# Layer 1's attention weights: six of eight blocks transposed in 32x32 squares on VectorE and moved by ScalarE and SyncE

## The chip, the cores and the metric

The kernel runs on one core of a Trainium2 chip. The core has five engines that work side by side, each through its own instructions in order: TensorE (PE, with its weight loads PEld), VectorE (DVE), ScalarE (ACT), GpSimd (POOL) and SyncE (SP), which here only issues transfers and relays signals. Sixteen DMA engines carry out the transfers that SP, ACT and POOL issue. The metric is the device time of one execution in microseconds (us), lower is better. Before the change it is 2416.36 us, the median of three runs (2415.96 to 2419.54).

## What is computed

The input is eight images of 256 channels and 1024 positions, all in float32. Layer 0 is eight-head attention with an output projection. Layer 1 works on the tokens t (1024 x 256 per image): first attention with one head and a residual, then a mixture of eight experts with two per token. The change is in layer 1's attention:

```python
t = t + _L1_attn_ref(_ln_t(t), L1_attn_W)

def _L1_attn_ref(x, W):
    xa = jnp.einsum('bnd,ed->bne', x, W)
    scores = jnp.einsum('bne,bme->bnm', xa, x)
    attn = jax.nn.softmax(scores, axis=-1)
    y = jnp.einsum('bnm,bmd->bnd', attn, x)
    return y
```

The softmax is over m, and the last product sums over m too. TensorE sums over the partitions, so a block of exponentials that was computed with n on the partitions must be turned, to have m there, before it can enter the last product.

## The kernel before, in words

The main loop takes the images one after the other. For each, `layer0` does the eight-head attention, `attend` does layer 1's attention, and `normed` with `dispatch` normalises, routes the tokens to experts and scatters them to DRAM. For the eighth image (b = 7) there is a difference: ahead of its `attend` the experts' products of the first seven images are computed, and during its `attend` and its own experts (`dense`) the results of the other seven are gathered from DRAM by POOL, added by DVE, turned by DVE and stored by SP (class `Results`, its places in `PLACES`).

`attend` normalises t to n1 (L645), turns it to nT (L648) and multiplies by W to xa (L655). Then it goes over eight blocks i of 128 tokens:

- `scores(i)`: four matmuls of 128x512 write the scores ps of block i to a PSUM tile (L670); DVE takes the negated row maximum nmax (L678); ACT writes the exponentials ex and their row sums to SBUF (L681). The ex tiles come from the pool `expp`, six buffers that share the tag "exps" with layer 0's exponentials.
- `mix(i)`: eight transposes of 128x128 on TensorE write the turned block pa to PSUM (L689); DVE copies it to SBUF as aT (L691); eight matmuls of 128x256 give py (L695); DVE scales by the reciprocal of the row sums and adds the residual (L699, L701).

The blocks are pipelined by one: `scores(i + 1)` is written ahead of `mix(i)`. The PSUM tiles ps and pa come from one pool of three (`ps_big`). Two calls of `fill` in the last block put pieces of the next image's projections (pv, pqk; L387, L328) into the stream, so that TensorE has work in the last waits; for b = 7 they are places of `Results`.

A scheduler places the instructions of each engine by its own estimates and adds the semaphores; it splits and interleaves groups. So before the change TensorE's stream in a middle block is: two matmuls of ps, eight of pa, two of the next ps, eight of py. What stands on SP's queue around `attend` is the load of later images (xT, L93; xs, L427) and the store of t (L1327).

Of the kernel before, what the change touches and what calls it, by code (L numbers as in the profile page):

```python
# [10 lines left out]
F32 = mybir.dt.float32  # L11
# [8 lines left out]
def kernel(  # L20
# [23 lines left out]
    nc = tc.nc  # L44
    P = 128
    B, C, S = x.shape
    E, D, FF = w1.shape
# [4 lines left out]
    NT = S // P  # L52
# [15 lines left out]
    expp = ctx.enter_context(tc.tile_pool(name="expp", bufs=6))  # L68
# [6 lines left out]
    def big(name):  # L75

        return ps_big.tile([P, 1024], F32, tag="big", name=name)

    def acc(name):

        return ps_acc.tile([P, 512], F32, tag="acc", name=name)
# [54 lines left out]
    for e in range(E):  # L136
# [30 lines left out]
        fill=0.0,  # L167
# [42 lines left out]
    SQ = 32  # L210
    NQ = P // SQ
# [40 lines left out]
    def layer_norm(t, dst, eps, name):  # L252
        return Norm(t, dst, eps, name).blocks(0, NT)

    def to_channels(t, dst, name):

        for cc in range(NCC):
            pt = big(f"pt_{name}_{cc}")
            for i in range(NT):
                nc.tensor.transpose(pt[:, ts(i, P)], t[:, i, ts(cc, P)], ident)  # L260
            copied = nc.vector.tensor_copy(dst[:, cc, :], pt)
        return copied
# [380 lines left out]
    def attend(b, t1, fill, tick=nothing):  # L643
        n1 = one.tile([P, NT, D], F32, tag="n", name=f"n1_{b}")
        layer_norm(t1, n1, 1e-5, f"a{b}")  # L645
        fill("norm 1")
        nT = one.tile([P, NCC, S], F32, tag="nT", name=f"nT_{b}")
        to_channels(n1, nT, f"n1_{b}")  # L648
        fill("normed 1")
        xa = one.tile([P, NCC, S], F32, tag="xa", name=f"xa_{b}")  # L650
        for ec in range(NCC):
            px = big(f"px_{b}_{ec}")
            for dc in range(NCC):
                for n in range(NH2):
                    nc.tensor.matmul(  # L655
                        px[:, ts(n, 512)],
                        WT[:, dc, ts(ec, P)],
                        nT[:, dc, ts(n, 512)],
                        start=(dc == 0),
                        stop=(dc == NCC - 1),  # L660
                    )
            tick(("xa", ec), nc.vector.tensor_copy(xa[:, ec, :], px))

        t2 = t1

        def scores(i):
            psc = big(f"ps1_{b}_{i}")
            for ec in range(NCC):
                for n in range(NH2):
                    nc.tensor.matmul(  # L670
                        psc[:, ts(n, 512)],
                        xa[:, ec, ts(i, P)],
                        nT[:, ec, ts(n, 512)],
                        start=(ec == 0),
                        stop=(ec == NCC - 1),
                    )
            nmax = small.tile([P, 1], F32, tag="nmax", name=f"nmax_{b}_{i}")
            tick(("max", i), nc.vector.tensor_reduce(nmax, psc, AX.X, ALU.max, negate=True))  # L678
            ex = expp.tile([P, 1024], F32, tag="exps", name=f"ex1_{b}_{i}")
            ssum = small.tile([P, 1], F32, tag="ssum", name=f"ssum_{b}_{i}")  # L680
            nc.scalar.activation(ex, psc, AF.Exp, bias=nmax, scale=1.0, accum_out=ssum)  # L681
            return ex, ssum

        def mix(i, ex, ssum):
            if i == NT - 1:
                fill("last weights")
            pt = big(f"pa_{b}_{i}")
            for m in range(NT):
                nc.tensor.transpose(pt[:, ts(m, P)], ex[:, ts(m, P)], ident)  # L689
            aT = two.tile([P, S], F32, tag="tr", name=f"aT_{b}_{i}")  # L690
            nc.vector.tensor_copy(aT, pt)  # L691
            ahead = fill("last products") if i == NT - 1 else None
            py = acc(f"py_{b}_{i}")
            for m in range(NT):
                nc.tensor.matmul(  # L695
                    py[:, :D], aT[:, ts(m, P)], n1[:, m, :], start=(m == 0), stop=(m == NT - 1)
                )
            rs = small.tile([P, 1], F32, tag="rs1", name=f"rs1_{b}_{i}")
            nc.vector.reciprocal(rs, ssum)  # L699
            with tc.issue_after(ahead.ins) if ahead else nullcontext():  # L700
                mixed = nc.vector.scalar_tensor_tensor(  # L701
                    t2[:, i, :], py[:, :D], rs, t1[:, i, :], ALU.mult, ALU.add
                )
            tick(("mixed", i), mixed)

        pending = None
        for i in range(NT):
            now = (i, *scores(i))
            if pending is not None:
                mix(*pending)  # L710
            pending = now
        mix(*pending)
        return t2


# [87 lines left out]
    def normed(b, t2, fill, tick=nothing, norm=None):  # L803

        if norm is None:
            n2 = one.tile([P, NT, D], F32, tag="n", name=f"n2_{b}")
            tick("normed", layer_norm(t2, n2, 1e-5, f"f{b}"))
        else:
            n2 = norm.dst
            tick("normed", norm.blocks(NT - 1, NT))  # L810
        fill("norm 2")
        nT = one.tile([P, NCC, S], F32, tag="nT", name=f"n2T_{b}")
        tick("turned", to_channels(n2, nT, f"n2_{b}"))

        nc.gpsimd.tensor_add(t2, t2, n2)  # L815
        fill("normed 2")
        l = logits(b, nT)
        return n2, nT, l
# [260 lines left out]
    class Results:  # L1079
# [94 lines left out]
        def tick(self, place, behind=None):  # L1174
            added, sent, stored = self.PLACES.get(place, (0, 0, 0))
            if added:
                with tc.issue_after(behind.ins):
                    for _ in range(added):
                        self.add()
            for _ in range(sent):  # L1180
                self.gather(behind)
            for _ in range(stored):
                if self.whole:
                    b, total, n = self.whole.pop(0)
                    store(b, total, n)
# [130 lines left out]
    for b in range(B):  # L1316
        xT = next_x
        if b + 1 < B:
            next_x = load_x(b + 1)
        if b > 0:  # L1320
            xs = load_squares(b)
        t1 = layer0(b, xT, begun, routing, xs)
        if b + 1 < B:
            begun = Begin(b + 1, next_x)
            t2 = attend(b, t1, begun.at)
            n2, _, l = normed(b, t2, begun.at)
            nc.sync.dma_start(groups[0].sums[b], t2)  # L1327
            routing = dispatch(b, n2, l, groups[0])
            continue
        experts(groups[0])  # L1330
        others = Results(groups[0])
        others.begin()
        norm = None

        def fill(place):

            nonlocal norm
            others.tick(place)
            if place == "last products":
                norm = Norm(t1, one.tile([P, NT, D], F32, tag="xa", name=f"n2_{b}"), 1e-5, f"f{b}")  # L1340
                return norm.blocks(0, NT - 1)

        t2 = attend(b, t1, fill, others.tick)
        dense(b, t2, norm, others.tick)
        assert others.added == len(others.units) and not others.whole
# [42 lines left out]
```

## Time and profile before

| What | Value |
|---|---|
| time, median of 3 | 2416.36 us |
| the profiled execution's own time | 2397.03 us |
| its span, first to last instruction | 2395.3 us |
| TensorE busy | 2353.9 us (98%) |
| VectorE, ScalarE, GpSimd busy | 64%, 39%, 18% |
| mean granted TensorE clock | 0.996 |
| DMA packets, data | 114778, 196.59 MB |

The profile shows one execution. Rows name the line, the engine, the operation and the tiles (out<-in), the shapes and the count, then the busy time and the mean of one, then the idle time ahead of them and what ended most of it. Float32 matmuls of this kernel appear as two MATMUL records each, the transposes as one. Records of matmuls overlap, so the pace of a group is read from the starts of its neighbours, not from the mean of one. The chain of waits is the work that ended last, followed back step by step. The profiled execution is 19 us shorter than the median of the timed runs; sums from the profile are differences and are put onto the median.

### The profile page before, as it was taken

To read this page: it belongs to the slowest core of one execution; us is meant where nothing else is said; L and a number is where in the kernel's file an instruction comes from. 1 tells how busy PE (TensorE), PEld (TensorE's weight loads), DVE (VectorE), ACT (ScalarE), POOL (GpSimd) and SP (SyncE) were. 2 spreads that over 40 slices of the span, in tenths; PEclk is the share of its full clock that TensorE was granted. 3 is DMA by queue.
4 is the path that set the end of the run, shared out by engine and by line. 5 is a ranking of instruction groups with operands and counts; after the bars stand their busy time and mean duration, and the time that the engine had idled before them with its cause. 6 is when DMAs were issued, how large, how long until landed. Compare 5 with 4: busy or idle time off the path is not lost.

```text
span 2395.3 us, 36813 instructions
## 1 busy us (share of the span) xinstructions
PE 2353.9 (98%) x13759; PEld 1313.9 (55%) x13759; DVE 1541.2 (64%) x3660; ACT 938.0 (39%) x1570; POOL 420.4 (18%) x391
## 2 busy tenths in 40 slices
PE   9999999999999999999999999999999999999898
PEld 3356534654466336633664356435653388887565
DVE  5775587457845785578647864787468763334776
ACT  3651266126611662156315641465136612221111
POOL 0000012000200020003000200020002234444663
PEclk9999999999999999999999999999999999999999
DMA  8993201010101010001000100100010256664454
GB/s 294 386 386 106 53 19 36 1 36 12 43 1 36 8 47 1 18 18 54 1 18 18 47 8 3 34 25 12 1 36 19 76 176 220 219 215 162 148 172 119
DMA packets 114778, 196.59 MB, mean 82 GB/s; under 512 B 15752, under 2 KB 58408, under 8 KB 112808
## 3 DMA queue, kind: packets, MB, share of 16 engines
q1 hardware_dynamic: 88504, 126.52, 16.0%
q0 software_dynamic: 25008, 67.20, 9.1%
q8 instruction: 109, 1.79, 0.3%
q10 hardware_dynamic: 1088, 0.52, 0.1%
q14 instruction: 69, 0.57, 0.1%
HBM read 108.88 MB, written 110.90 MB: 92 GB/s over the span
## 4 chain that ended last, share of the span: by engine, by line
PE 90%; DVE 5%; DMA 2%; ACT 1%; issue 1%; POOL 0%; SPq 0%; DVEq 0%; ACTq 0%; POOLq 0%
PE po L545 19%; PE psc L468 18%; PE py L695 8%; PE ps L670 7%; PE pqk L350 7%; PE pr L636 5%; PE pv L387 4%; PE ph L1025 4%; PE pe L1050 4%; PE pdh L1254 2%; PE px L655 2%; PE pdy L1278 2%; PE pa L689 2%; PE pqk L328 2%; PE px L1015 1%
## 5 line engine op out<-in xcount | busy, mean ns | idle before, releaser
L509 ACT ACTIVATE ex<-psc,nmax 128x1024 f32<-128x1024 f32 x512 | 570.5, 1115 | 304.1 <-DVE scrap L492 220.4
L468 PE MATMUL psc<-qk,qk 64*64 64x512 f32 x4096 | 577.4, 593 | 10.3 <-ACT ex L509 10.3
L545 PE MATMUL po<-ex,vs 64*64 64x512 f32 x4096 | 573.2, 592 | 1.3 <-DVE vs L525 0.3
L492 DVE TENSOR_SCALAR_CACHE_REDUCE scrap<-psc,nmax 128x512 f32<-128x512 f32 x512 | 384.5, 751 | 149.0 <-PE psc L468 121.8
L483 DVE TENSOR_REDUCE nmax<-psc 128x1 f32<-128x512 f32 x512 | 350.7, 685 | 9.3 <-PE psc L468 9.3
L468 PEld LDWEIGHTS psc<-qk,qk 64*64 64x64 f32 x4096 | 180.7, 132 | 285.9 <-ACT ex L509 138.3
L545 PEld LDWEIGHTS po<-ex,vs 64*64 64x64 f32 x4096 | 177.6, 132 | 273.0 <-issue 81.2
L695 PE MATMUL py<-n,aT 128*128 128x256 f32 x1024 | 236.3, 384 | 2.9 <-DVE aT L691 2.9
L670 PE MATMUL ps<-nT,xa 128*128 128x512 f32 x512 | 236.0, 592 | 0.0
L695 PEld LDWEIGHTS py<-n,aT 128*128 128x128 f32 x1024 | 190.5, 190 | 66.1 <-DVE aT L691 41.8
L888 POOL DMA_INDIRECT rows<-n,d_at x112 | 108.8, 972 | 654.4 <-DVE nmax L483 654.1
L681 ACT ACTIVATE ex<-ps,nmax 128x1024 f32<-128x1024 f32 x64 | 71.3, 1115 | 348.0 <-DVE nmax L678 333.5
L815 POOL TENSOR_TENSOR t<-t,n 128x2048 f32<-128x2048 f32 x8 | 36.3, 4532 | 924.0 <-DVE n L242 924.0
L350 PE MATMUL pqk<-xT,wqkv 128*128 128x512 f32 x384 | 171.2, 599 | 0.0
L701 DVE SCALAR_TENSOR_TENSOR t<-py,rs,t 128x256 f32<-128x256 f32 x64 | 30.9, 483 | 192.7 <-PE py L695 192.7
L670 PEld LDWEIGHTS ps<-nT,xa 128*128 128x128 f32 x512 | 93.5, 190 | 81.2 <-issue 75.1
L350 PEld LDWEIGHTS pqk<-xT,wqkv 128*128 128x128 f32 x384 | 71.0, 190 | 99.9 <-issue 77.8
L1134 POOL DMA_INDIRECT yk<-y,yat x112 | 111.0, 991 | 70.1 <-issue 27.1
L636 PEld LDWEIGHTS pr<-wo,res 128*128 128x128 f32 x512 | 120.7, 331 | 3.7 <-ACT res L563 3.7
L636 PE MATMUL pr<-wo,res 128*128 128x256 f32 x512 | 121.6, 398 | 0.3 <-ACT res L563 0.3
L387 PE MATMUL pv<-wqkv,xT 128*128 128x512 f32 x256 | 120.3, 599 | 1.2 <-DVE v L395 1.0
L315 ACT ACTIVATE qk<-pqk,b_qks 128x512 f32<-128x512 f32 x124 | 85.6, 691 | 88.9 <-PE pqk L350 79.8
(189 smaller groups left out, 2477.8 us busy)
## 6 DMA issues: line engine op xcount, KB each, us to landing
rows<-wb SPq DMA_DIRECT2D x7, 8192.0 KB, 51.7
y<-yb SPq DMA_DIRECT2D x63, 256.0 KB, 2.3
xs<-in_x_dram SPq DMA_DIRECT2D x64, 128.0 KB, 4.0
out_dram<-oT SPq DMA_DIRECT2D x60, 128.0 KB, 2.9
xT<-in_x_dram SPq DMA_DIRECT2D x7, 1024.0 KB, 4.8
sums<-t SPq DMA_DIRECT2D x7, 1024.0 KB, 3.9
o<-sums SPq DMA_DIRECT2D x7, 1024.0 KB
wpack<-in_L_ffn_w_dram SPq DMA_DIRECT2D x4, 1024.0 KB
```

What stands on the lines that cost most here:

```text
L350: mm = nc.tensor.matmul(pq[:, ts(n, 512)], wqkv[:, cc, t, ts(g, P)], xT[:, cc, ts(n, 512)], start=(cc == 0), stop=(cc == NCC - 1),)
L387: nc.tensor.matmul(pv, self.xT[:, cc, ts(i, P)], wqkv[:, cc, 2, :], start=(cc == 0), stop=(cc == NCC - 1),)
L468: mm = nc.tensor.matmul(pss[at, h][ts(c, DK), ts(n, 512)], k[r, j * P + c * DK : j * P + (c + 1) * DK], q[r, ts(n, 512)], start=True, stop ...
L483: firsts[at, h] = nc.vector.tensor_reduce(nmax, pss[at, h][:, ts(0, 512)], AX.X, ALU.max, negate=True)
L492: seconds[h] = nc.vector.tensor_scalar(scrap, pss[at, h][:, ts(1, 512)], -1.0, nmaxes[at, h], ALU.mult, ALU.min, accum_out=nmax,)
L509: nc.scalar.activation(ex, pss.pop((at, h)), AF.Exp, bias=nmaxes.pop((at, h)), scale=1.0, accum_out=sums[at][:, h : h + 1],)
L545: mm = nc.tensor.matmul(po[n][ts(h, DK), :], vss[at][keys, h, :], exps[at, h][keys, ts(n, 512)], start=(j == 0 and turn == 0), stop=(j == ...
L636: nc.tensor.matmul(pr[:, :C], own(res[:, g, :], i), wo[:, g, :], start=(g == 0), stop=(g == NPAIR - 1))
L670: nc.tensor.matmul(psc[:, ts(n, 512)], xa[:, ec, ts(i, P)], nT[:, ec, ts(n, 512)], start=(ec == 0), stop=(ec == NCC - 1),)
L695: nc.tensor.matmul(py[:, :D], aT[:, ts(m, P)], n1[:, m, :], start=(m == 0), stop=(m == NT - 1))
L888: scatter = nc.gpsimd.indirect_dma_start(out=view[:, :], out_offset=bass.IndirectOffsetOnAxis(ap=ats[k][:, i : i + 1], axis=0), in_=n2[:, ...
L1134: ins = nc.gpsimd.indirect_dma_start(out=self.slot(at)[:, k, :], out_offset=None, in_=self.group.y[:, :], in_offset=bass.IndirectOffsetOnAxis(
```

## The change

For the blocks 1 to 6, `turn` takes the place of TensorE's transposes. VectorE turns each 32x32 square of the 128x1024 block in place among the squares (`nc.vector.transpose`, into sq). That leaves each square turned inside, but in the wrong group of 32 partitions. Sixteen moves per block then bring the squares to their places in aT, each from 32 partitions to 32 partitions, 8 runs of 32 floats (128 B) per partition: eight are copies on ACT, eight are transfers issued by SP. sq and aT are two more tiles of the pool `expp`. Blocks 0 and 7 keep the old way (`turn_now`). The order of writing changes too: the product of block i is written two blocks behind its scores instead of one, block 0's after the scores of block 2, and the last three products (5, 6, 7) stand after the scores of block 7, with `fill("last weights")` after product 5 and block 7's transposes ahead of product 6.

```diff
-        def mix(i, ex, ssum):
-            if i == NT - 1:
-                fill("last weights")
+        def turn(i, ex):
+            sq = expp.tile([P, S], F32, tag="exps", name=f"sq_{b}_{i}")
+            nc.vector.transpose(sq, ex)
+            aT = expp.tile([P, S], F32, tag="exps", name=f"aT_{b}_{i}")
+            to = aT.rearrange("p (m a q) -> p a m q", a=NQ, q=SQ)
+            since = sq.rearrange("p (m k q) -> p k m q", k=NQ, q=SQ)
+            for a in range(NQ):
+                for k in range(NQ):
+                    move = nc.sync.dma_start if (a + k) % 2 else nc.scalar.copy
+                    move(to[ts(k, SQ), a], since[ts(a, SQ), k])
+            return [aT[:, ts(m, P)] for m in range(NT)]
+
+        def turn_now(i, ex):
             pt = big(f"pa_{b}_{i}")
             for m in range(NT):
                 nc.tensor.transpose(pt[:, ts(m, P)], ex[:, ts(m, P)], ident)
             aT = two.tile([P, S], F32, tag="tr", name=f"aT_{b}_{i}")
             nc.vector.tensor_copy(aT, pt)
+            return [aT[:, ts(m, P)] for m in range(NT)]
+
+        def mix(i, aT, ssum):
             ahead = fill("last products") if i == NT - 1 else None
             py = acc(f"py_{b}_{i}")
             for m in range(NT):
                 nc.tensor.matmul(
-                    py[:, :D], aT[:, ts(m, P)], n1[:, m, :], start=(m == 0), stop=(m == NT - 1)
+                    py[:, :D], aT[m], n1[:, m, :], start=(m == 0), stop=(m == NT - 1)
                 )
...
-        pending = None
+        pending = []
         for i in range(NT):
-            now = (i, *scores(i))
-            if pending is not None:
-                mix(*pending)
-            pending = now
-        mix(*pending)
+            ex, ssum = scores(i)
+            if 0 < i < NT - 1:
+                ex = turn(i, ex)
+            pending.append((i, ex, ssum))
+            if i == 2:
+                first, ex, ssum = pending.pop(0)
+                mix(first, turn_now(first, ex), ssum)
+            elif i > 2:
+                mix(*pending.pop(0))
+        fill("last weights")
+        (last, ex, ssum) = pending.pop()
+        ex = turn_now(last, ex)
+        mix(*pending.pop())
+        mix(last, ex, ssum)
```

NQ is 4 and SQ is 32. In the changed kernel L688 is the square transpose, L695 the moves, L702 and L704 the old transposes and their copy, L711 the products.

## The prediction

> **What bounds the kernel now.** I read the chain of waits of the whole page first. TensorE carries 90% of it, and the transposes that the change takes out (pa, L689) are 2%.
>
> ```profile
> PE 90%; DVE 5%; DMA 2%; ACT 1%; issue 1%; POOL 0%; SPq 0%; DVEq 0%; ACTq 0%; POOLq 0%
> ```
>
> Then the chain inside one `attend` (second image; start, duration in us, engine, tile, line, count):
>
> ```profile
> 448.23 3.45 PE ps L670 x8
> 451.70 1.24 DVE nmax L678
> 453.00 1.28 ACT L681
> 454.30 1.21 ACT ex L681 x2
> 455.56 1.09 PE pa L689 x8
> 456.65 1.72 PE ps L670 x4
> 458.37 3.45 PE py L695 x16
> 461.82 1.72 PE ps L670 x4
> 463.54 0.87 PE pa L689 x8
> 464.41 1.72 PE ps L670 x4
> 466.13 3.58 PE py L695 x16
> ```
>
> From the second block on only TensorE is in it. A block takes 7.89 us (pa at 463.54, 471.42 and 479.31): 0.87 pa, 3.44 ps, 3.58 py. The stretch from the first ps (448.23) to the end of the last py (515.18) is 66.95 us. So TensorE time removed here is time of the end, if nothing later takes its place.
>
> Third, the groups that serve as prices:
>
> ```profile
> L434 DVE STREAM_TRANSPOSE t<-xs 128x1024 f32<-128x1024 f32 x16 | 32.0, 2060 | 0.0
> L681 ACT ACTIVATE ex<-ps,nmax 128x1024 f32<-128x1024 f32 x64 | 71.3, 1115 | 348.0 <-DVE nmax L678 333.5
> ```
>
> A square transpose of a whole block costs 2.06 us; ScalarE idles 348 us ahead of its 64 exponentials, so it has room. Fourth, the transfers. The eight xs loads at 503 us have the shape of one block's transfers (8 transfers, 256 packets each), but 512 B packets from HBM; the second line is the half microsecond from 10.0 us, which holds only packets of 256 B or less (mostly b_v):
>
> ```profile
> q1 hardware_dynamic: 2176, 1.05, 57.3%
> q1 hardware_dynamic: 396, 0.10, 88.1%
> 502.99 3.76 SPq L427 DMA_DIRECT2D xs<-in_x_dram  x8
> ```
>
> A packet's engine time: 0.573 x 10 us x 16 engines / 2176 = 42 ns at 512 B; 0.881 x 0.5 x 16 / 396 = 17.8 ns at 256 B. Issuing: 3.76 / 8 = 0.47 us each.
>
> **What the Trainium skill says.** "VectorE: DVE Perf Modes", The three transpose paths: VectorE turns only 32x32 blocks, so the squares must still be moved; the kernel's own L434 and L1190 agree, since they store by quadrant. "ScalarE: Activation LUTs", Table sets: copies are in every set, so the copies cost no table load; the trace agrees (res copies stand among exponentials without one). "DMA: Bandwidth & Descriptors", Specifications: below 512 B a transfer does read-modify-write; the same page, Why small descriptors are slow (HBM only), says SBUF to SBUF does not suffer. The 17.8 ns speak against a penalty on reading small packets, but no transfer from SBUF to SBUF is in this trace: this is the largest unknown.
>
> **The change part by part.** I place the changed program's TensorE order for the second to seventh image on a clock (ps 3.45 us, py 3.45, pa 0.87, a pv of two matmuls 1.72): ps0, ps1, ps2, pa0, 3/4 ps3, py0, 1/4 ps3, 1/4 ps4, py1, 3/4 ps4, py2, ps5, py3, ps6, py4, ps7, py5, pv2, pa7, py6, pv3, py7.
>
> *Removed from TensorE*: six pa, 6 x 0.87 = 5.2 us; the start bubble (from 451.70 to 455.56 are 3.86 us, of which ps1 hides 3.45), 0.4 us; and 0.13 us that a py takes longer behind its copy, seven times, 0.9. Check: 8 x 3.45 + 8 x 3.45 + 2 x 0.87 + 2 x 1.72 = 60.4 against 66.95, 6.5 us less.
>
> *Added waits on TensorE*: py of a turned block now waits for eight transfers, mostly landed. For the price of landed waits: VectorE's first n of an image waits for eight landed scatters and starts 0.20 us after the reciprocal ends (435.85 to 436.05), without them 0.03 (266.76 to 266.79). 0.17 x 6 = 1.0 us, behind which the rest of py and the next ps queue. I charge it all; it is nothing if TensorE's queue runs ahead.
>
> *VectorE*: the copy of pa (1.22) goes, a transpose (2.06; 1.1 if the contiguous form ran at the copy's pace per element) comes. Per block: 1.22 nmax + 2.06 + 0.16 + 0.48 + 0.43 + 0.18 = 4.5 us, hidden under TensorE's 6.9.
>
> *ScalarE*: eight copies of 32 x 256. lT's copy of 256 elements took 0.373 us; two res copies in a row 1.06 against 0.59 for one, so in a row one costs 0.12 less. 0.37 + 7 x 0.26 = 2.2 to 8 x 0.40 = 3.2 us (0.40: the SBUF-to-SBUF wqkv copy of 512 elements, 0.614, less 256 x 0.83 ns, the rate of the "ScalarE: Activation LUTs" page); I take 2.5. The exponentials of the next block queue behind these copies, which wait for sq, which waits for this block's exponentials: a loop of 1.30 + 2.06 + 2.5 + 0.15 = 6.0 us (6.7 at the upper end), under TensorE's 6.9. Cover gone, every us above 6.9 is paid in five blocks.
>
> *Transfers*: 8 issues of 0.47 = 3.8 us per block on an otherwise waiting SP queue; the xs loads behind them need ps7 anyway. Engines: 2176 packets / 16 = 136 each, 2.4 us at 17.8 ns, 5.7 at 42. I take 30 ns, 4.1 us, hidden. Landing: 2.3 us (the median of y's stores, 256 KB) to 4.7 (xs); with seven issues ahead the last lands 5.6 us after sq.
>
> *Latency of a block*, from the end of ps: 0.2 + 1.23 nmax, 1.3 ex, 2.06 sq, 5.6, hand-overs 0.15: 10.5 us. On the clock ps3 ends at 18.1 and py3 starts at 31.9: 13.8 us. 3.3 to spare, of which VectorE's order (nmax behind the previous sq, a scaling and a statistic) and ScalarE's (ex behind copies) eat about 2. For a few first blocks the margin is 1 us; I charge 0.6 us per image.
>
> *Buffers*: ex, sq and aT rotate through the six of `expp`; some copies of ScalarE wait for the transfers that read sq two blocks earlier, landed by then. PSUM gets freer.
>
> So per image 6.5 - 1.0 - 0.6 = 4.9, six images: 29.4 us. *First image*: here VectorE's fourth transpose stands behind the scaling of py1, after ps6, and SP is held until 211.4 us by the packing of weights (sq of block 1 is ready at about 209.5); I take 2 of the 4.9 (0 to 5). *Last image*: POOL's gathers and SP's stores already use 53% of the DMA engines from 2185 to 2262 us, and VectorE is busy 57.4 of 77 us; six transposes instead of copies add 5. At 30 ns the transfers would need 4.1 / 0.47 = 8.7 us per block against 7.9: a loss of some 5, less its saving of 4.9. I take +1 (-5 to +25). Sum: -29.4 - 2 + 1 = -30.4. The profiled execution would span 2365 us; on the median, 2386.
>
> **The rivals.**
> *Transfers by rate, slower.* If a 128 B packet costs more, the transfers set the pace. sq1 is ready at 11.8 us on the clock; 48 transfers of 17 packets per engine, then 1.2 landing, py6, pv3, py7: the image ends at 21.6 + 816p us. It exceeds 66.95 from p = 56 ns. For: the skill's read-modify-write. Against: 17.8 and 42 ns. At 74 ns (twice the 37 ns of the final 512 B stores: 0.211 x 12 x 16 / 1088) it ends at 82.0, +15 per image, +120: 2536. Place: TensorE before py1 to py6.
> *Transfers by latency, nothing left.* ps of block k to py of block k spans two blocks. If the last lands 3 us later than I take it, the loop is 10.5 + 2 + 3.3 = 15.8, 7.9 us per block, as before: 2416. For: xs landed up to 8.3 us after issue. Against: those read HBM, in a queue.
> *ScalarE as the bound, half the gain.* At 0.50 us per copy the loop is 1.30 + 2.06 + 4.0 + 0.15 = 7.5, 0.6 above 6.9 in five blocks: 3.0 of the 4.9 are lost. 30.4 - 18 = 12.4: 2404. Against: every copy row in the trace.
> That the transposes are not gone is excluded: the changed program's TensorE list has two pa per image.
>
> **How the numbers follow.** Likeliest case 0.58 (2370 to 2400), ScalarE 0.12 (2400 to 2411), latency 0.08 (2412 to 2421), rate 0.14 (2425 to 2600), transfers late enough in latency or in the last image to lose 5 to 40 us 0.08. A difference under 0.2%, 4.8 us, can't be told from none in this kernel. Faster 0.58 + 0.12 = 0.70, same 0.08, slower 0.22. The range goes from 2369 (upper bounds: every image 6.5 us, 0.04 below) to 2450, which takes in the late cases and the first part of the rate case and leaves some 0.14 above; the likeliest case alone is 2370 to 2400.
>
> **What would show it.** Right: `attend` of the middle images about 62 us from first ps to last py; TensorE idle before L711 under 1 us per block; ScalarE moves at 0.3 to 0.4 us; some 104,000 more packets (48 x 2176) at 20 to 42 ns. Wrong: idle of TensorE before L711 ended by transfers (rate if the DMA row reads 9 in `attend`, latency if it reads 5 or less), or idle before ps ended by ex (ScalarE's loop). A last image over 10 us longer would be the collision with gathers.

## The result and the profile after

The changed kernel takes 2383.74 us (median of 4 runs, 2381.21 to 2386.16), the kernel before 2416.16 us (2415.91 to 2419.54): ratio 0.986, 95% interval 0.985 to 0.988, 32 us less. The forecast was 2386. The time agrees; below, several of its terms don't.

The chain of waits of the whole page, kernel after. TensorE still carries 90%. A share that was not there before is put down to another core or an unknown queue, although the program runs on one core; the experiments come back to it:

```profile
PE 90%; DVE 5%; DMA 1%; issue 1%; ACT 1%; another core or an unknown queue 1%; SPq 0%; DVEq 0%; ACTq 0%; POOLq 0%
```

The chain inside one `attend`, second image, kernel after (start, duration in us, engine, tile, line, count):

```profile
447.28 10.30 PE ps L670 x24
457.58 0.87 PE pa L702 x8
458.46 2.58 PE ps L670 x6
461.03 3.45 PE py L711 x16
...
475.69 3.43 PE ps L670 x8
479.12 3.45 PE py L711 x16
482.57 3.43 PE ps L670 x8
486.00 3.45 PE py L711 x16
```

From the first ps on, TensorE alone is in it. A block is 3.43 + 3.45 = 6.88 us instead of 7.89, with nothing between the two. Measured on TensorE's timeline from the first ps to the end of the last py, the stretch is 60.44 us in each of the six middle images, against 67.12 before.

The groups that replace the prices of the forecast: first the new ScalarE copies (busy us, mean ns, idle before them), then the instructions that write sq (ns min/median/max), then those that write aT by transfer (time to issue one, same columns).

```profile
L695 ACT COPY aT<-sq 32x256 f32<-32x256 f32 x384 | 154.4, 402 | 77.3 <-DVE sq L688 47.4
```

```profile
L688 DVE STREAM_TRANSPOSE sq<-ex x48: 1210/1245/1334, 207.2 to 2208.9; 128x1024 f32<-128x1024 f32 x48
```

```profile
L695 SPq DMA_DIRECT2D aT<-sq x384: 4/609/1707, 212.7 to 2214.7; - x192
```

The contiguous transpose costs 1.245 us, not the 2.06 us of the rows that store by quadrant; a copy 0.402 us, with 3.30 us for eight in a row, so they do not overlap; an issue 0.61 us in the median, with 0.65 us from one to the next. And the DMA row of the same image from 458 to 494 us (busy tenths of the 16 engines, then packets, MB and share):

```profile
DMA  0224324032422223324302242240031423401224
...
q1 hardware_dynamic: 12238, 1.48, 27.0%
```

0.270 x 36 us x 16 engines / 12,238 packets = 12.7 ns per packet of 128 B, under the lower end (17.8) of the forecast. No slice of the row reads above 4: the engines are far from full.

### The profile page after: what moved, and what is told of

It reads as the page before. It is cut to its first block, busy times and chain, and to the rows that moved or that the text cites. A ratio compares the mean times of both kernels' runs of the same rounds, so it can differ in the third digit from the quotient of the medians.

```text
span 2382.3 us, 37255 instructions
## 1 busy us (share of the span) xinstructions
PE 2316.6 (97%) x13375; PEld 1280.4 (54%) x13375; DVE 1537.0 (65%) x3660; ACT 1091.7 (46%) x1954; POOL 421.7 (18%) x391
## 4 chain that ended last, share of the span: by engine, by line
PE 90%; DVE 5%; DMA 1%; issue 1%; ACT 1%; another core or an unknown queue 1%; SPq 0%; DVEq 0%; ACTq 0%; POOLq 0%
PE po L545 19%; PE psc L468 19%; PE py L711 9%; PE ps L670 9%; PE pqk L350 7%; PE pr L636 5%; PE pv L387 4%; PE ph L1052 4%; PE pe L1077 4%; PE pdy L1305 2%; PE px L655 2%; PE pdh L1281 2%; PE pqk L328 2%; PE px L1042 1%
## 5 line engine op out<-in xcount | busy, mean ns | idle before, releaser
L509 ACT ACTIVATE ex<-psc,nmax 128x1024 f32<-128x1024 f32 x512 | 570.0, 1114 | 306.8 <-DVE scrap L492 220.3
L711 PE MATMUL py<-n,aT 128*128 128x256 f32 x1024 | 234.2, 382 | 5.5 <-DVE aT L704 4.6
L670 PE MATMUL ps<-nT,xa 128*128 128x512 f32 x512 | 228.8, 592 | 0.2
L711 PEld LDWEIGHTS py<-n,aT 128*128 128x128 f32 x1024 | 195.9, 192 | 56.6 <-issue 24.0
L695 ACT COPY aT<-sq 32x256 f32<-32x256 f32 x384 | 154.4, 402 | 77.3 <-DVE sq L688 47.4
L678 DVE TENSOR_REDUCE nmax<-ps 128x1 f32<-128x1024 f32 x64 | 78.0, 1219 | 84.9 <-PE ps L670 80.4
```

The lines of the kernel that those rows point to most:

```text
L509: nc.scalar.activation(ex, pss.pop((at, h)), AF.Exp, bias=nmaxes.pop((at, h)), scale=1.0, accum_out=sums[at][:, h : h + 1],)
L670: nc.tensor.matmul(psc[:, ts(n, 512)], xa[:, ec, ts(i, P)], nT[:, ec, ts(n, 512)], start=(ec == 0), stop=(ec == NCC - 1),)
L695: move(to[ts(k, SQ), a], since[ts(a, SQ), k])
L711: nc.tensor.matmul(py[:, :D], aT[m], n1[:, m, :], start=(m == 0), stop=(m == NT - 1))
```

## The experiments

Each kernel left a trace, and the differences between images are finer there than in the total. The table cuts each profiled execution at the first ps of an image (us): the first image, the mean of the second to sixth (to the next image's first ps), the seventh (up to the last image's first ps), and from there to the end.

| kernel | first | 2nd to 6th | seventh | last to end | median of runs | ratio to before, 95% |
|---|---|---|---|---|---|---|
| before (the execution that the forecast read) | 250.3 | 248.1 | 503.0 | 203.8 | 2416.2 | |
| before_again | 250.3 | 248.1 | 504.9 | 216.9 | 2412.1 | 1.000 (0.9995 to 1.0012) |
| after_again | 250.7 | 241.4 | 496.8 | 227.5 | 2380.1 | 0.986 (0.984 to 0.987) |
| order_only | 249.6 | 247.3 | 505.6 | 219.8 | 2409.1 | 0.997 (0.996 to 0.998) |
| half | 245.9 | 244.7 | 500.6 | 219.0 | 2389.6 | 0.990 (0.988 to 0.992) |
| last_old | 249.5 | 241.4 | 495.9 | 218.4 | 2372.0 | 0.983 (0.981 to 0.985) |
| last_old2 | 249.5 | 241.4 | 496.6 | 219.1 | 2371.6 | 0.983 (0.982 to 0.984) |
| last_dve | 249.5 | 241.4 | 497.8 | 221.1 | 2374.0 | 0.984 (0.983 to 0.985) |
| last_sp | 249.3 | 241.4 | 498.3 | 227.3 | 2379.4 | 0.986 (0.985 to 0.988) |
| last_actq | 249.5 | 241.4 | 497.2 | 220.3 | 2374.8 | 0.984 (0.983 to 0.985) |
| act12 | 247.2 | 246.3 | 504.0 | 225.9 | 2405.1 | 0.996 (0.994 to 0.997) |
| sp12 | 254.2 | 249.2 | 506.8 | 230.3 | 2435.5 | 1.008 (1.007 to 1.010) |
| deep3_7 | 257.8 | 247.5 | 503.5 | 222.2 | 2416.8 | 1.001 (1.000 to 1.002) |

### Order or transposes: order_only and half

order_only writes the products two blocks behind the scores, with every block transposed by TensorE; half moves blocks 1, 3 and 5 in squares in that order. The added lines of the loop (the removed ones and its end left out):

```diff
+            if waiting is not None:
+                j, jex, jsum = waiting
+                pending.append((j, turn_now(j, jex), jsum))
+                waiting = None
+            if i in ():            # half: (1, 3, 5)
+                pending.append((i, turn(i, ex), ssum))
+            else:
+                waiting = (i, ex, ssum)
+            if i >= 2:
+                mix(*pending.pop(0))
...
```

> All eight blocks transposed by TensorE, as before the change, but written in the changed order: the transposes one block behind the scores, the products two blocks behind. Theory (the gain is the TensorE time of the transposes): only the start bubble and the 0.13 us per product go, 1.3 us per image, 8 images: 9 to 11 us faster than before, 2406. Rival (the gain is the deeper order, which hides the chain of maximum, exponential and copy): more than half of the 32 us, 2400 or less.

> Blocks 1, 3 and 5 moved in squares, blocks 0, 2, 4, 6 and 7 by TensorE, in the order of order_only. Theory: three of six transposes of 0.87 us are gone, so the time lies midway between order_only and the changed kernel: about 2395. Rival (order): the same as order_only and as the changed kernel within 5 us. If the moves themselves cost TensorE something that grows with their density, it lies nearer to the changed kernel than midway, 2388 or less.

order_only is 2409.1 us, 7 less than before on that chip (2415.9), not the 9 to 11 expected: the deeper order is a small part. The stretch of a middle image goes 67.12 (before), 66.38 (order_only), 63.75 (half), 60.44 (after): 0.74 for the order, then 2.63 for the first three transposes, 0.88 each, which is the 0.87 us of the pa row. The last three give 3.31: 2.6 for themselves, and 0.65 at the first pa. In order_only and half it stands behind the scores of block 1, idles 0.43 us for its exponential and takes 1.09 us; in the changed kernel it stands behind the scores of block 2, without a wait, and takes 0.87. So the saving in the middle images is mainly TensorE time of transposes, and it adds up block by block. In total time half did not lie midway (2395) but at 2389.6. The table says where: in the six middle images it saves less than after_again, in the first and in the last more. Something at both ends charges for the squares.

### The same kernels once more: after_again and before_again

Both kernels as they are.

> The changed kernel once more, nothing edited. It asks whether VectorE's idle times in the last image (5.3 us ahead of the copy of block 0, 6.6 us ahead of the scaling of block 6) belong to the program or to one execution. If they belong to the program: about 2384 us, and the stretch of the last image from its first ps to its last py is again about 74 us, against 67 in the kernel before, with the same two waits. If they are chance: about 2384 us too, but the waits are gone or stand elsewhere, and the last image's stretch is under 70 us.

> The kernel before once more, nothing edited. Its profiled execution lasted 2397 us, 19 us less than the median of its runs, and its last stretch (from the last image's first ps to the end of the span, 204 us) is 14 to 27 us shorter than in all kernels run so far, the ones with the old last image among them. If that execution was an exception: an execution of about 2416 us shows idle times of VectorE in the last image or behind it whose releaser the trace does not name, and a last stretch of 215 to 225 us; the difference between the kernels then lies in the images before it. If the stretch is again 204 us in an execution of 2397 us: the changed orders of writing bring these idle times in.

after_again: 2380.1 us; the last image's stretch is 79.9 us (73.8 in the first execution of after), and VectorE again idles 5.4 us ahead of the copy of block 0 and 6.3 us ahead of a scaling. before_again, an execution of 2411.88 us, has such idle times too. VectorE's waits of before_again, us in total, times, longest (two lines of the answer), then SyncE's:

```profile
DVE t L1287 <- remote: 8.1, 4, 2.7
DVE t L701 <- remote: 3.1, 1, 3.1
```

```profile
SPq L1208 <- remote: 11.0, 1, 11.0
```

"remote" is the view's word for a releaser that it cannot name. The packed traces show more: in before_again, after and after_again the semaphore of all these waits of over half a microsecond is the one that TensorE's matmuls update, and the update came 1.6 to 6.0 us after the recorded end of the last matmul that makes one. So by this record VectorE, ScalarE and SyncE waited for TensorE, not for another core; whether TensorE was late there or its recorded ends are early stayed open. The idle times occur in both kernels, from the last image on. The execution of the kernel before that the forecast was made from (2397 us) has none of these waits, was 15 to 19 us below the kernel's ordinary time, and its last part is 203.8 us instead of 216.9. What follows is that the page of before gave a last part some 13 us too short, and that the ordinary last part is 217 to 220 us, to which after's 227.5 and 231.1 (first profile of after) must be compared.

### The last image: last_old, last_old2, last_dve, last_sp, last_actq

last_old (and, the same kernel again, last_old2) gives the last image its former loop:

```diff
+        if b == 7:
+            held = None
+            for i in range(NT):
+                now = (i, *scores(i))
+                if held is not None:
+                    mix(held[0], turn_now(held[0], held[1]), held[2])
+                held = now
+            fill("last weights")
+            mix(held[0], turn_now(held[0], held[1]), held[2])
+            return t2
```

> The last image alone goes back to the loop and the TensorE transposes of the kernel before; images 0 to 6 keep the squares. Theory (the squares collide in the last image with gathers, stores and the combining work of VectorE, and lose there what one image gains and more): 8 to 15 us faster than the changed kernel, 2369 to 2376. Rival (the last image's idle times are chance, and the squares gain there as elsewhere): 0 to 6 us slower than the changed kernel, 2384 to 2390.

> The kernel with the old last image once more, as the base for the two below on the same chip: 2372 us, ratio to the kernel before 0.983.

2372.0 and 2371.6 us. The first is 8.1 us faster than after_again on the same chip (the ranges of the runs, to 2377.0 and from 2378.5, do not touch), and the kernel is the fastest of this study. The gain is in the last part, 218.4 instead of 227.5. So the squares lose 8 us there on balance, against some 6.7 that they save in another image. Three kernels add one load each to last_old's last image, into tiles that nobody reads (the added line of each; the loop around it left out):

```diff
+                    nc.vector.transpose(spare, now[1])                # last_dve
...
+                                nc.sync.dma_start(to[ts(k, SQ), a], since[ts(a, SQ), k])   # last_sp, where (a + k) % 2
...
+                                nc.scalar.dma_start(to[ts(k, SQ), a], since[ts(a, SQ), k]) # last_actq, where (a + k) % 2
```

> The kernel with the old last image, and in that image six square transposes by VectorE more (blocks 1 to 6, into tiles that nobody reads): it adds VectorE's work of the change, 6 x 1.25 us less nothing, without its transfers and copies. If VectorE's order sets the last image (transposes between the combining work and the scalings): 5 to 8 us slower than the base, about 2379. If the loss comes from the transfers or the copies: within 3 us of the base.

> The kernel with the old last image, and in that image the 48 transfers of the change more (squares of ex, untransposed, into tiles that nobody reads), on SyncE's queue: it adds the change's transfers alone. If they collide with the gathers, or hold SyncE's stores of the outputs back: 5 to 10 us slower than the base, about 2379. If not: within 3 us of the base.

> As last_sp (the old last image with 48 transfers of 32 KB more that nobody reads), but these are issued by ScalarE on its own queue instead of SyncE's. last_sp was 8 us slower than its base. If it was the order on SyncE's queue (stores of outputs behind transfers that wait for exponentials): within 3 us of the base, 2372 to 2375. If the transfers collide with the gathers on the DMA engines, or share a limit that does not depend on the issuing engine: again 6 to 10 us slower, about 2380.

VectorE's six transposes cost 2.4 us (the runs of the two kernels overlap, so this may be nothing), the 48 transfers 7.8 us in the median and 8.2 in the last part. That is as much as the loss on balance; if the transposes that leave TensorE save their 6.7 us here too (an estimate from the other images), some 5 us more are lost to something that was not singled out. Issued from ScalarE's queue the same transfers cost 1 to 3 us (ratio 0.984 against 0.983 for the base and 0.986 for last_sp; last part 220.3, 219.1 and 227.3). The same packets cross the same DMA engines beside the same gathers, so their rate is not it; the queue that they stand in is. SyncE's timeline in the last image, last_old2, then last_sp (start, length to the last of the group, line, transfer, count):

```profile
2172.41 37.57 SPq L1234 DMA_DIRECT2D out_dram<-oT  x16
```

```profile
2161.73 30.30 SPq L735 DMA_DIRECT2D spare<-ex  x32
2192.12 3.04 SPq L1242 DMA_DIRECT2D out_dram<-oT  x4
2195.26 5.20 SPq L735 DMA_DIRECT2D spare<-ex  x8
```

The first store of an output goes out 21.9 us after the image's first ps in last_old2 (2150.5), 39.9 us after it in last_sp (2152.2): it stands behind 32 transfers, the last of which wait for the exponentials of block 4. In the changed kernel itself (first execution) it is 31.3 us, behind 16 transfers. That the last image waits for its own moves as well is in after_again's chain there:

```profile
2214.33 0.61 SPq L695
2214.99 2.71 DMA aT<-sq
2217.79 4.97 PE py L711 x16
```

Which wait hands the late stores on to the end of the kernel was not singled out. Nor was the part of TensorE's own pace: in the first execution of after it idles 4.6 us ahead of the first product of this image, the granted clock is 0.5 for 6.8 us from 2167.3 us, and this product takes 5.88 us where the others take 3.62.

### How near the two movers are to their limits: act12 and sp12

The 16 moves of a block are split 12 to 4, one way and the other, in all images.

```diff
-                    move = nc.sync.dma_start if (a + k) % 2 else nc.scalar.copy
+                    move = nc.sync.dma_start if (a + k) % 4 == 3 else nc.scalar.copy   # act12
+                    move = nc.sync.dma_start if (a + k) % 4 else nc.scalar.copy        # sp12
```

> The changed kernel with the 16 moves of a block split 12 copies on ScalarE to 4 transfers, in all images. From the changed kernel's trace: exponentials 1.30, transpose 1.25, a copy every 0.41 us, hand-overs 0.15. If ScalarE's loop binds as the prediction's rival has it, a block takes 1.30 + 1.25 + 12 x 0.41 + 0.15 = 7.6 us instead of the 6.9 of TensorE; the first exponentials of a turned block start 8.4 us after the first ps, six loops later (54 us) come those of block 7, then its transposes and the last three products: the stretch of a middle image is 65 us instead of 60.4, and the time 2414 (2405 to 2420). If the loop is not what binds (copies overlap, or the next exponentials go ahead of them): stretch and time as in the changed kernel, 60.4 and 2382.

> The changed kernel with 4 copies on ScalarE to 12 transfers per block, in all images. From the changed kernel's trace eight transfers are issued in 4.95 us, 0.62 each, and a block's packets need only 1.7 us of the engines. If issuing binds: 12 x 0.62 = 7.4 us per block, six blocks from 11 us after the first ps make 55.6, 2 us to land and the last three products make a stretch of 66 us instead of 60.4: 2420 (2408 to 2430). If what counts is the packets' own time on the DMA engines (12 x 256 x 13 ns / 16 = 2.5 us): stretch 60.4, time 2382.

act12 is 2405.1 us. VectorE's timeline in its second image (start, duration, idle before it in brackets):

```profile
469.49 1.25 DVE L688 STREAM_TRANSPOSE sq<-ex 128x1024 f32<-128x1024 f32 x1 [4.15 <-ACT ex L681]
...
476.99 1.25 DVE L688 STREAM_TRANSPOSE sq<-ex 128x1024 f32<-128x1024 f32 x1 [4.10 <-ACT ex L681]
```

A block takes 7.50 us: 1.30 + 1.25 + 4.95 for twelve copies, with hand-overs of nearly nothing. VectorE idles 4.1 us for the exponential, which stands behind the copies. TensorE then idles once, ahead of the transposes of block 7, its only line of waits in that image:

```profile
PE pa L702 <- ACT ex L681: 3.3, 1, 3.3
```

The stretch is 64.3 to 67.2 us (expected 65). The total is 9 us under the expected 2414; the first image alone is 3.5 us shorter than after_again's. Why was not shown: TensorE's order of work differs there too.

sp12 is 2435.5 us, slower than before and 5 us above the expected range. SyncE's line for its second image:

```profile
462.68 48.36 SPq L695 DMA_DIRECT2D aT<-sq  x72
```

48.36 / 72 = 0.67 us per transfer, 8.1 us per block, and the stretch is 67.5 to 68.5 us (expected 66). One issue takes 0.61 us and the next follows 0.65 us after its start, as at eight per block. The packets' own time, 12 x 256 x 12.7 ns / 16 = 2.4 us per block, would not have shown. So the issuing instruction is the limit of the transfers, and both movers at eight moves (5.8 us ScalarE's loop, 5.2 us SyncE's issues) sit below TensorE's 6.9 with little to spare. By an estimate from these prices ScalarE binds from ten to eleven copies ((6.9 - 2.55) / 0.41 = 10.6), SyncE from ten to eleven transfers (6.9 / 0.65 = 10.6).

### A version that was to beat the best: deep3_7

```diff
...
-            if 0 < i < NT - 1:
+            if i < NT - 1:
                 ex = turn(i, ex)
             pending.append((i, ex, ssum))
-            if i == 2:
-                first, ex, ssum = pending.pop(0)
-                mix(first, turn_now(first, ex), ssum)
-            elif i > 2:
+            if i > 2:
                 mix(*pending.pop(0))
...
```

with seven buffers in `expp`, one more product after the loop, and last_old's last image.

> A version meant to beat both: images 0 to 6 with block 0 in squares too, the products three blocks behind the scores and seven buffers instead of six for ex, sq and aT; the last image in the old way. One transpose of 0.87 us less on TensorE in each of seven images: 6 us faster than the kernel with the old last image, 2366. If an exponential that now waits for the product three blocks back (their tile shares its buffer) comes too late: the same or slower, 2372 to 2385, with TensorE idle ahead of ps or py in the middle images.

2416.8 us: the whole gain is gone, and neither expectation (2366, or 2372 to 2385) holds. TensorE's waits over the whole of it (us, times, longest):

```profile
PE pa L702 <- ACT ex L681: 19.6, 7, 6.3
PE pt_n L260 <- DVE n L242: 11.0, 8, 2.0
```

against 3.0 and 2.1 for the same two in last_old2. Products that used to stand between scores are now left for the end of an image, the pv that covered the end have moved forward, and the last block's transposes and the normalization wait in the open. TensorE also waits for exponentials ahead of ps, 3.9 us in ten places. That accounts for 29 of the 45 us to last_old2; the rest was not traced. That the order of the products is the cause is argued from these waits: the order, the turned block 0 and the seventh buffer were changed together.

## Why the prediction was right, and where its terms were not

*Removed from TensorE: 6.5 us per image.* Right: 6.68 in the stretch, 6.7 from image to image. Its parts were shown one by one: six transposes of 0.88, 0.74 for the order, 0.65 at the first pa.

*Added waits on TensorE, 1.0 us per image, and 0.6 us for the first blocks.* This step failed. A block is 6.88 us, its ps and py and nothing else, and TensorE has no wait at all in the second image. The clause "it is nothing if TensorE's queue runs ahead" was the one to take: a price read on VectorE was carried to TensorE, where it does not appear. TensorE's weight loads do run ahead (the first for the py at 479.12 us starts at 478.53, under the last ps); that this hides the price was not tested. 1.6 x 6 = 9.6 us too pessimistic.

*First image, -2 us.* Mis-sized: -0.8 and +0.4 in the two executions. Of its two reasons the first held. Lines of the timelines of VectorE, ScalarE and TensorE, first execution of after:

```profile
229.61 0.48 DVE L717 SCALAR_TENSOR_TENSOR t<-py,rs,t 128x256 f32<-128x256 f32 x1 [2.16 <-PE py L711]
230.01 1.24 DVE L688 STREAM_TRANSPOSE sq<-ex 128x1024 f32<-128x1024 f32 x1
...
231.28 3.30 ACT L695 COPY aT<-sq 32x256 f32<-32x256 f32 x8 [6.58 <-DVE sq L688]
...
248.05 1.12 PE L702 MATMUL pa<-ident,ex 128*128 128x128 f32 x8 [2.96 <-ACT ex L681]
248.98 3.58 PE L387 MATMUL pv<-wqkv,xT 128*128 128x512 f32 x4
```

The fourth transpose stands behind the scaling of py1, and ScalarE idles 6.6 us for it. From there ScalarE's loop sets the pace (copies from 231.28, 237.12 and 243.47 us), the exponential of block 7 comes late, and TensorE idles 3.0 us ahead of that block's transposes. Around the end of this wait the granted clock fell to 0.5, for 3.4 us from 249.0 us (in after_again for 6.8 us from 247.1), and the four pv behind it took 3.58 us where they take 1.88 in the kernel before; the forecast had no term for that. The second reason, SyncE's late start, is there (first transfer at 212.7 us) but costs nothing that shows: TensorE waits for no transfer in this image. The chain names one, ahead of the fifth transpose:

```profile
233.86 1.99 DMA aT<-sq
235.85 1.23 DVE sq L688
```

But this transpose started at 235.84 us, 0.03 us after the end of the exponential that it reads, as the first one does; releasers are inferred, and here the inference is wrong. In half and act12 this image is shorter (245.9 and 247.2), with a different order on TensorE as well; which of the differences does it was not tested.

*Last image, +1 us (-5 to +25).* Mis-sized: +8.1 against last_old in the median. The place was right and the mechanism half: the forecast priced the DMA engines' share at 30 ns per packet, and last_sp against last_actq puts most of it on the queue that SyncE's stores stand in.

*The sum.* From before_again to after_again: first image +0.4, five images of 6.7, the seventh 8.1, the last part +10.6: -0.4 + 33.5 + 8.1 - 10.6 = 30.6 us. -30.4 was forecast. The six images gave 12 us more than forecast (9.6 of them the waits that did not come), and the first and the last image together 12 us less. These errors cancelled: the agreement of the total is partly luck.

*Prices.* The transpose 1.245 us (2.06 taken, 1.1 as the alternative), eight copies 3.30 (2.5 taken, 3.2 the upper end), so the sum for ScalarE's loop stays 6.0 (5.8 in the trace, from copies to copies at 458.02 and 463.86 us), by two errors of opposite sign. The saving for copies in a row, read from the res copies, did not appear. An issue is 0.61 us (0.47), a packet 12.7 ns (30), and in the middle images the last piece lands 2.0 us after its issue, 6.6 us after sq (medians) instead of 5.6. With the shorter transpose the latency of a block is then 10.7 us against 10.5, inside the 13.8 us between ps3 and py3.

*From the profiled execution to the median.* The step "would span 2365; on the median, 2386" failed in its first half: the execution spanned 2382.3. The offset of 19 us was no constant between profile and run: in before_again, 15 us longer, 13 of the 15 stand in the last part, with the idle times that the recorded execution of before lacks.

*The rivals.* By rate: out, 12.7 ns against the 56 ns where it would decide. This agrees with the Trainium skill, "DMA: Bandwidth & Descriptors", Why small descriptors are slow (HBM only), by which transfers from SBUF to SBUF are spared the penalty: 12.7 ns is less than the 17.8 and 42 ns of the larger packets in the trace before. Larger packets from SBUF to SBUF were not run. By latency: out in the middle images, no wait of TensorE there. ScalarE as the bound: out at eight copies (0.402 us each, not 0.50), but the mechanism is real, as act12 shows. That no table is loaded between copies and exponentials, from the Trainium skill's "ScalarE: Activation LUTs", Table sets, held: in the second image ScalarE loads a table ahead of the first exponential and behind the last, and none among the exponentials and copies between them.

## What to carry to other kernels

In the middle images work taken from the engine that sets the end paid about its own time; its new carriers needed a spare queue and a loop below that engine's period, and here the loop was set by the number of issues and copies (0.65 and 0.41 us each), not by the packets' own time (2.4 us per block even at twelve transfers). Look at the images at both ends separately: in the last one the same queue already carries stores that others wait for, and the change was better left out of it. A forecast should rest on more than one profiled execution, since one can lack idle times that most have.

## What was not expected of the hardware

- 128 B packets from SBUF to SBUF took 12.7 ns of an engine each, less than the packets of up to 256 B, mostly a load, in the kernel before (17.8).
- A 128 x 1024 transpose in squares took 1.245 us where both sides are contiguous, 2.06 us where the kernel before stores by quadrant.
- ScalarE's copies of 32 partitions followed each other every 0.41 us without overlap; issuing a transfer of 256 packets took SyncE 0.61 us, at eight and at twelve per block.
- Idle times of VectorE, ScalarE and SyncE of up to 11 us each, waits for the semaphore of TensorE's matmuls that end 1.6 to 6.0 us after the recorded end of the last one, stand from the last image on in the executions of both kernels, all but the first one of before. In the first of after the granted TensorE clock was 0.59 from 2225 to 2245 us, where TensorE was busy 6.9 of 20 us. Cause and order of the two stayed open.
- In the first image of both executions of after the granted clock was 0.5 for 3.4 and 6.8 us around the end of TensorE's one wait of 3.0 us; the four pv behind it took 3.58 and 3.62 us instead of 1.88.
